# A four-layer residual kernel: the first pair's projections in 27 slots for 31, and two key batches asked for at other slots

## The chip, the cores and the metric

The kernel runs on one core of one Trainium2 chip. The metric is the device time of one execution in microseconds (us), and a lower time is better. All arithmetic is in 32-bit floats. The engines are called by short names: PE is TensorE, DVE is VectorE, ACT is ScalarE, POOL is GpSimd, and SP is SyncE, which here only issues transfers.

## What is computed

The input x has 64 batches of 32 rows of 512 columns (2048 rows in all). Four layers each add their result to x:

```python
x = x + _L0_cond_ref(x, itok_B_0_15, L0_cond_weights)       # mixes the 32 rows of a batch by one of 16 matrices
x = x + _L1_cond_ref(x, itok_B_6_15, base_weight, base_bias, lora_A_w, lora_B_w)   # linear, with a low-rank part
x = x + _L2_cond_ref(x, Wq, Wk, Wv, Wo, q_norm_w, k_norm_w, k_cache, v_cache, block_table, cache_seqlens)
x = x + _L3_cond_ref(x, L3_cond_weights, itok_B_0_15)       # mixes rows again
```

L2 is attention with a paged cache. Cut to what matters:

```python
q = rope(rmsnorm(x @ Wq.T))          # 32 heads of 128
k = rope(rmsnorm(x @ Wk.T)); v = x @ Wv.T      # 8 heads of 128
k_all = concat(k_cache[block_table], k)        # 512 cached keys (16 pages of 32) and 32 new ones
scores = q @ k_all.T / sqrt(128), cached keys from cache_seqlens on masked
out = softmax(scores) @ v_all, then @ Wo.T
```

Four query heads share one key head.

## The kernel before

The 2048 rows are 16 tiles of 128 rows (four batches each). The eight key heads are two groups of four. A step is one tile of one group, so there are 32 steps. A unit is one batch of a step, so there are 128 units, and each unit has four slots, one for each key head. A slot is the clock in which the program is written out: slot 0 is the first softmax slot, slot 511 the last, and slots -42 to -1 hold the first stage. Inside a slot a fixed order of parts is run (`slot`): "fetch" and "pool" first, then the scores of this slot's head, the products with values of the slot three before, the transposes of the probabilities of the slot two before, then "out", "pe", "take", "late", "power", up to three pieces of the norms (`norm_piece`), "turn", "dve", "keep", "act" and "store". A call is entered into the plan with `at(slot, part, function)`. Engines do not wait for slots: each runs its own queue in this order and waits only for what its instruction needs, so that the slot sets the order of the work and not its time.

The first stage (L0 and L1) runs tile by tile, two slots a tile: `home` is the tile's first slot. At `home` x is turned and mixed on PE (`turn_x`, L450, tile x1T_ps), at `home + 1` come the low-rank part (`ranks`, L465, h_ps) and three of five matmuls of L1 (`linear`, L481, l_ps), at `home + 2` the last two and the addition of the bias on DVE (`add`, L429), at `home + 3` the result is transposed (`turn_out`, L434, x2T_ps) and stored. For every second tile the sums of two tiles that the projections need (`sums`, L507 to L511, tiles x_12 and x_34) are made at `home + 4` on DVE and stored at `home + 5` (`store_sums`, L528, xS). The stores of the last three tiles go through POOL's queue, those before through SP's.

Projections take two tiles (a pair) at once, by a scheme of seven products for eight. For each pair there are three blocks: one for keys and values (KV), two for queries. A block has seven products of two matmuls each (`Block.project`, L664, 128x512, tile proj_ps, or a scores buffer s_ps for some of the first pair's), and a tuple of 14 slots says when each matmul is issued. There is one proj_ps buffer, so a product can start only when DVE (`add`, L676) or ACT (L684, the first product of a block) has taken the one before. Four results of a query block and two of the KV block go through a norm and a rotation: ACT squares them (L720), POOL takes a power (L725, L727), DVE does four pieces (`scale` L732, `straight` L739, `swapped` L751, `sum` L761), PE turns the heads (`turn`, L766, head_ps) and ACT keeps them (L778) as qT or kT_new. The value results are stored to memory (`store_values`, L706, vn) through SP's queue. `norm_piece` hands out the DVE pieces: at most two to a slot, three in every fourth, less what the takes and the block sums (`block_sum`, L628) have booked in `busy`.

For each unit SP asks for the 16 key pages (`Unit.__init__`, L796 to L804, kT, two buffers, 16 transfers of 64 KB), after having loaded the page numbers into registers. POOL makes the mask of the unit (`mask`, L819, tile pen) and gathers four tiles of values (L105, v_sb). The scores (L848, L851) go to the one s_ps buffer that the scores have; one instruction of DVE masks them and takes the maximum (L856), ACT does the exponential (L867) and a scaling (L873), PE transposes (L890, pT_ps), DVE copies (L892) and PE multiplies with the values (L900, o_ps).

The memory pools of the first stage are closed at slot -2 (`first.close()`), and the pools of the softmax (among them pen and v_sb) are opened in their place. The pool of the turned cache pages (`start_pool`) is closed a slot before the first keys are asked for, and the key buffers are opened there.

The variable `home` in the projections' loop is 32*(i-1) - 1 for pair i, so -33 for pair 0 and -1 for pair 1. The second part of the kernel, the product with Wo and L3, is not touched.

## Time and profile before

| | us |
|---|---|
| three timed runs | 2434.95, 2435.93, 2442.22 |
| median | 2435.93 |
| profiled execution, its own time | 2435.27 |
| its span, first to last instruction | 2433.5 |
| first matmul of PE starts | 10.00 |
| first scores (slot 0) start | 178.64 |
| scores of slot 4 and slot 8 start | 193.19 and 207.28 |

The page gives each engine's busy time and its share of the span, and cuts the span into 40 slices of 61 us, so the first stage fills slices 1 to 3. The waits list, for an engine, what it waited for with the total, the number of waits and the longest, in us. The timeline gives instructions in order of time: start, duration, engine, line, operation, what it writes and reads, and in brackets the idle time of the engine before it with what ended it. "SPq" rows are transfers being issued by SP: their duration is the issue's, not the transfer's. Two matmul instructions with one result show as x2; their ends are modelled, and the next one can start about 0.16 us before the end that the row shows. That drain counts as idle time when the next matmul has to wait.

### The profile page before, as it was taken

How to read it: one execution, taken by the hardware profiler on the slowest of the kernel's cores; microseconds unless marked ns; L12 is line 12 of the kernel's file. 1: busy time of each engine (PE TensorE's matmuls, PEld its weight loads, DVE VectorE, ACT ScalarE, POOL GpSimd, SP SyncE). 2: the span in 40 equal slices, each digit the busy share in tenths (PEclk: the TensorE clock that was granted, in tenths of full speed). 3: DMA queues.
4: the chain of work that ended last, by engine and by line, in shares of the span. 5: the costliest groups of instructions: out<-in, count | busy, mean ns of one | idle time of the engine just before them, and what ended most of it. 6: DMA issues, size and time to landing. Idle time of an engine off the chain costs nothing.

```text
span 2433.5 us, 47110 instructions
## 1 busy us (share of the span) xinstructions
PE 2398.2 (99%) x13792; PEld 1864.7 (77%) x13792; DVE 1651.9 (68%) x3555; ACT 1398.8 (57%) x4006; POOL 1230.5 (51%) x1269
## 2 busy tenths in 40 slices
PE   7999999999999999999999999999999999999999
PEld 4557777777777777777777777777777788888887
DVE  5557877777777777887777777777777856333222
ACT  2246767777777777777777777777676764000000
POOL 3336566655655666665656656666656663000000
PEclk9999999999999999999999999999999999999999
DMA  8766666676767677766666666566667874333221
GB/s 278 255 219 198 192 191 197 190 205 187 207 182 208 181 218 235 242 186 192 177 187 176 186 174 190 176 185 179 187 182 223 259 249 152 109 114 126 87 90 59
DMA packets 461055, 452.09 MB, mean 186 GB/s; under 512 B 67728, under 2 KB 383760, under 8 KB 457216
## 3 DMA queue, kind: packets, MB, share of 16 engines
q1 hardware_dynamic: 404960, 269.05, 36.7%
q0 software_dynamic: 55024, 179.25, 24.3%
q8 instruction: 111, 1.82, 0.3%
q14 instruction: 144, 1.18, 0.2%
q10 hardware_dynamic: 816, 0.79, 0.1%
HBM read 380.73 MB, written 76.55 MB: 188 GB/s over the span
## 4 chain that ended last, share of the span: by engine, by line
PE 93%; DMA 2%; ACT 1%; DVE 1%; issue 1%; SPq 1%; POOL 0%; ACTq 0%; DVEq 0%; POOLq 0%
PE proj_ps L664 23%; PE o_ps L900 18%; PE out_ps L1360 15%; PE s_ps L848 10%; PE pT_ps L890 9%; PE s_ps L851 9%; PE head_ps L766 3%; PE l_ps L481 3%; PE o_ps L913 1%; DMA o<-oT 1%; PE s_ps L883 1%; PE x1T_ps L450 1%; PE h_ps L465 1%; PE proj_ps L1174 1%; PE mix_ps L1378 1%
## 5 line engine op out<-in xcount | busy, mean ns | idle before, releaser
L105 POOL DMA_INDIRECT v_sb<-v,v_rows x512 | 544.4, 1063 | 357.1 <-PE o_ps L900 244.2
L900 PE MATMUL o_ps<-pT,v_sb 128*128 128x128 f32 x4096 | 623.8, 275 | 0.4 <-DMA v_sb<-v,v_rows 0.4
L900 PEld LDWEIGHTS o_ps<-pT,v_sb 128*128 128x128 f32 x4096 | 578.0, 191 | 27.4 <-DMA v_sb<-v,v_rows 0.6
L867 ACT ACTIVATE sm<-sm,top 128x544 f32<-128x544 f32 x512 | 380.9, 744 | 344.3 <-DVE top L856 341.5
L856 DVE CUSTOM_DVE_ANT_0 sm<-s_ps,pen 128x544 f32<-128x544 f32 x512 | 369.4, 722 | 111.5 <-PE s_ps L851 105.0
L873 ACT ACTIVATE sm<-sm,share 128x512 f32<-128x512 f32 x512 | 369.9, 722 | 100.2 <-DVE share L872 88.7
L892 DVE COPY pT<-pT_ps 128x512 f32<-128x512 f32 x512 | 353.3, 690 | 54.9 <-PE pT_ps L890 15.6
L848 PE MATMUL s_ps<-kT,qT 128*128 128x288 f32 x1024 | 334.5, 408 | 5.4 <-DMA kT<-kT 3.8
L890 PE MATMUL pT_ps<-ident,sm 128*128 128x128 f32 x2048 | 309.8, 274 | 4.6 <-ACT qT L778 3.1
L676 DVE TENSOR_TENSOR raw<-proj_ps,raw 128x512 f32<-128x512 f32 x332 | 224.4, 688 | 130.0 <-PE proj_ps L664 129.7
L851 PE MATMUL s_ps<-kT,qT 128*128 128x256 f32 x1024 | 304.7, 379 | 0.2 <-DMA kT<-kT 0.2
L848 PEld LDWEIGHTS s_ps<-kT,qT 128*128 128x128 f32 x1024 | 179.1, 190 | 152.7 <-issue 131.1
L819 POOL TENSOR_SCALAR pen<-key_f,seq_f 128x544 f32<-128x544 f32 x128 | 283.6, 2216 | 13.3 <-DMA kT<-kT 2.0
L890 PEld LDWEIGHTS pT_ps<-ident,sm 128*128 128x128 f32 x2048 | 238.7, 142 | 8.9 <-ACT qT L778 4.7
L720 ACT ACTIVATE sq<-raw 128x128 f32<-128x128 f32 x640 | 198.4, 310 | 74.9 <-DVE raw L676 59.8
L851 PEld LDWEIGHTS s_ps<-kT,qT 128*128 128x128 f32 x1024 | 194.5, 190 | 54.2 <-issue 0.6
L105 POOL DMA_INDIRECT mix_rows<-in_w,cond_rows x32 | 36.7, 1148 | 345.9 <-DVE mix_diag L170 299.8
L872 DVE RECIPROCAL share<-total 128x1 f32<-128x1 f32 x512 | 83.9, 164 | 181.1 <-ACT sm L867 167.0
L725 POOL TENSOR_SCALAR ss<-ss 128x4 f32<-128x4 f32 x160 | 39.4, 246 | 309.8 <-ACT sq L720 306.4
L1410 ACT COPY p<-out_ps 128x256 f32<-128x256 f32 x7 | 2.6, 372 | 333.1 <-PE out_ps L1360 333.1
L664 PE MATMUL proj_ps<-sum,x 128*128 128x512 f32 x380 | 188.0, 597 | 0.0
L727 POOL TENSOR_TENSOR rstd<-ss,minus_half 128x4 f32<-128x4 f32 x160 | 168.5, 1053 | 13.3
(175 smaller groups left out, 3570.7 us busy)
## 6 DMA issues: line engine op xcount, KB each, us to landing
kT<-kT SPq DMA_DIRECT2D x2048, 64.0 KB
o_in<-o SPq DMA_DIRECT2D x28, 1024.0 KB
o<-oT POOLq DMA_DIRECT2D x69, 256.0 KB, 3.0
o<-oT SPq DMA_DIRECT2D x58, 256.0 KB
v<-in_kv_cache SPq DMA_DIRECT2D x32, 256.0 KB
kT<-page_rows SPq DMA_DIRECT2D x32, 256.0 KB
vn<-raw SPq DMA_DIRECT2D x32, 256.0 KB
v_sb<-v,v_rows POOLq DMA_INDIRECT x512, 4.3
```

The source lines that it names most:

```text
L105: nc.gpsimd.indirect_dma_start(out=dst, out_offset=None, in_=table, in_offset=bass.IndirectOffsetOnAxis(ap=index, axis=0),)
L664: nc.tensor.matmul(self.ps, lhsT=self.pair.x[x][:, c if x == "b" else half.start + c, :], rhs=blocks(self.b)[w][:, c, :], start=(c == 0), ...
L819: nc.gpsimd.tensor_scalar(self.pen, key_f, seq_f[:, self.b : self.b + 1], BIG, ALU.is_ge, ALU.mult)
L848: nc.tensor.matmul(ps[:, first:HID], lhsT=q, rhs=self.kT[:, :n1, k, :], start=True, stop=True)
L851: nc.tensor.matmul(ps[:, HID : first + LA], lhsT=q, rhs=self.kT[:, n1:, k, :], start=True, stop=True)
L856: nc.vector.tensor_tensor_reduce(out=sm, in0=ps[:, first : first + LA], in1=self.pen, scale=1.0, scalar=3e38, op0=ALU.add, op1=ALU.min, ac ...
L867: nc.scalar.activation(sm, sm, AF.Exp, bias=top, scale=-1.0, accum_out=total)
L873: nc.scalar.activation(sm[:, :L], sm[:, :L], AF.Copy, scale=share)
L890: nc.tensor.transpose(ps[:, c, :], self.sm[k][:, c * P : (c + 1) * P], ident)
L892: nc.vector.tensor_copy(pT, ps)
L900: nc.tensor.matmul(o_of[self.s, k][:, self.j, :], lhsT=self.v[c][:, k * D : (k + 1) * D], rhs=self.pT[k][:, c, :], start=(self.j == 0 and ...
L1360: nc.tensor.matmul(ps[:, :HALF], lhsT=o[:, i, :], rhs=w[i // REP][:, i % REP, :], start=(i == 0), stop=(i == KG * REP - 1),)
```

## The change

The change does five things.

- The 14 matmuls of each block of pair 0 are laid into nine slots (`DENSE`) for ten, and the blocks begin 9 slots after each other, so that the first pair's projections take slots -33 to -7, where they took -33 to -3. One block sum is made at slot 14 of the pair for 17.
- The KV block of pair 1 begins two slots earlier, at slot -3, and still ends at slot 8.
- Up to slot -5, three norm pieces may run in a slot, where two or three could.
- The L1 of tiles 10 to 15 is one slot later, so the last tile's `home` is -8 for -9.
- The first unit's keys are asked for at slot -8 for -6, the second unit's at slot -1 for -3. The pool of the turned pages is closed two slots earlier with it.

```diff
         def norm_piece(slot):
-            if not pieces or pieces[0][0] > slot or busy.get(slot, 0) >= 2 + (slot % 4 == 1):
+            room_for = 3 if slot < -4 else 2 + (slot % 4 == 1)
+            if not pieces or pieces[0][0] > slot or busy.get(slot, 0) >= room_for:
                 return
...
+        DENSE = (0, 0, 1, 1, 2, 3, 4, 4, 5, 6, 7, 7, 8, 8)
...
                 (0, (10, 11, 12, 12, 13, 14, 15, 15, 16, 17, 18, 18, 19, 20)),
                 (1, (21, 21, 22, 23, 24, 24, 25, 26, 27, 27, 28, 29, 30, 30)),
             ):
+                if i == 0:
+                    slots = [(0, 9, 18)[(KV, 0, 1).index(b)] + w for w in DENSE]
+                elif i == 1 and b == KV:
+                    slots = (-2, -2, -1, -1, 0, 1, 2, 3, 4, 5, 7, 8, 9, 9)
                 slots = [home + w for w in slots]
...
-                    (17, 0, 4),
+                    (17 if i else 14, 0, 4),
...
-        ready = -6
+        ready = -8
         for t in range(NT):
-            home = -WINDOW - AHEAD - 6 + 2 * t
+            home = -WINDOW - AHEAD - 6 + 2 * t + (t > 9)
...
-            at(KG * (u - 1) if u > 1 else ready + 3 * u, "fetch", make, unit_of, u, Unit, u)
+            at(KG * (u - 1) if u > 1 else (ready, -1)[u], "fetch", make, unit_of, u, Unit, u)
```

## The prediction

> **What bounds the kernel now.** I read the page's first two parts, then TensorE's waits, then the timelines of all queues around the place that the change touches.

> ```profile
> PE 2398.2 (99%) x13792; PEld 1864.7 (77%) x13792; DVE 1651.9 (68%) x3555; ACT 1398.8 (57%) x4006; POOL 1230.5 (51%) x1269
> PE   7999999999999999999999999999999999999999
> PEclk9999999999999999999999999999999999999999
> ...
> PE x1T_ps L450 <- DVE mix_diag L421: 10.0, 1, 10.0
> PE s_ps L848 <- DMA kT<-kT: 3.8, 2, 2.2
> PE pT_ps L890 <- ACT qT L778: 3.1, 6, 1.6
> PE proj_ps L664 <- DVE raw L676: 1.6, 1, 1.6
> ```

> TensorE (PE) is busy for 99% of the span at full clock, and the change takes no matmul away. So it can only fill or open holes in PE's queue. In program order nothing differs behind about slot 10, some 40 us after the first scores (178.64 to 218.00). What counts is the idle time up to there: 10.0 us before the first matmul (untouched) and small holes, most of them near the first scores.

> ```profile
> 163.63 1.02 PE L481 MATMUL l_ps<-b_rows,hT 128*128 128x512 f32 x2
> 170.30 0.63 PE L766 MATMUL head_ps<-ident,rot_a 128*128 128x128 f32 x4 [0.48 <-DVE rot_a L761]
> 174.27 1.98 PE L664 MATMUL proj_ps<-wv,x_a 128*128 128x512 f32 x4 [1.62 <-DVE raw L676]
> 178.64 0.72 PE L848 MATMUL s_ps<-kT,qT 128*128 128x288 f32 x2 [1.66 <-DMA kT<-kT]
> 181.34 0.75 PE L848 MATMUL s_ps<-kT,qT 128*128 128x288 f32 x2 [0.68 <-DVE top L856]
> 186.79 0.63 PE L890 MATMUL pT_ps<-ident,sm 128*128 128x128 f32 x4 [1.37 <-issue]
> ...
> 173.07 1.08 POOL L528 DMA_DIRECT2D xS<-x  x2
> 178.39 2.12 POOL L819 TENSOR_SCALAR pen<-key_f,seq_f 128x544 f32<-128x544 f32 x1 [2.00 <-DMA kT<-kT]
> ...
> 166.85 10.16 SPq L804 DMA_DIRECT2D kT<-kT  x16
> 178.21 9.95 SPq L804 DMA_DIRECT2D kT<-kT  x16
> 193.14 9.79 SPq L804 DMA_DIRECT2D kT<-kT  x16
> ```

> Columns: start, duration, instruction, and in brackets the idle time before it with what ended it. E is the moment when PE is through with the last tile's L1: 163.63 plus two issues of 0.43, 164.49. Slot 4's scores start at 193.19, E+28.70. PE's work between, by start-to-start distances of the rows (projection matmul 0.86, four transposes 0.44, a score pair 0.92, a tile of o_ps or pT_ps 0.44): 14 projections 12.04, 5 head turns 2.20, x2T 0.44, four scores 3.68, pT and o 1.76; 20.12 in all. **The holes are 8.58 us.** That is what the change can win here. From E back to the first projection (37.41) they are 2.6 us, 1.39 at 41.40 and 0.70 at 78.00 the only large ones, and from 193.19 to slot 8 (207.28) some 0.3.

> The pen (the mask) matters beside the keys: it lies in memory that the first stage gives up, and in program order it waits for every transfer of that stage, the two xS stores of the last tile latest. Its 178.39 is 4.8 us after the second store's issue (173.61), and the first softmax (DVE, 180.55) starts as it ends.

> **The change part by part.** Projections: Pair 0's 42 matmuls, with their takes (DVE, ACT), squares, powers, turns and two vn stores, come up to four slots earlier and end at slot -7. Before E there are then 7 more matmuls (6.02) and 3 more heads (1.32): 7.3 us moved, not saved. Between E and slot 4 there remain 9 projections 7.74, 3 heads 1.32, x2T 0.44, scores 3.68, pT and o 1.76: 14.94. The hole at 78.00 goes, as the product behind the double take gets a slot's work between. Against it, twice a product follows the one before over x1T alone (0.89) where drain, take and two handovers need 0.16+0.04+0.69+0.05 = 0.94; I take 0.15 each. Dense stage: -0.4, with ends -0.7 and (five such holes of 0.7) +2.8. The earlier block sum (4 at 14 for 17) and the third piece a slot only reorder DVE, which is 50 to 60% busy there by the page's slices; cost nothing while that holds.

> L1 of tiles 10 to 15 a slot later: No projection now follows tile 15's last L1 matmul, so PE meets DVE's chain naked. Times from E, DVE steps by the rows 174.14 to 176.85 (straight 0.60, swapped 0.78, sum 0.61, scale 0.72; a rotation 2.71): the add runs 0.20 to 0.88, x2T starts at 0.93 (hole 0.94). The rest of one rotation (0.78, then 0.67) ends at 2.26: head at 2.31 (hole 0.94). A whole rotation more ends at 5.0: head at 5.05 (hole 2.30). Pair 1's first value product 5.49 to 7.21; ACT's copy (0.59) has to empty the one proj_ps buffer, so the second starts at 8.12 (hole 0.91); head to 10.28; the take ends at 10.73 and lets the next product start at 10.78 (hole 0.50). First scores at 11.64, next product done at 13.42. Before, block 1's last products filled this stretch.

> Pen: DVE starts tile 15's sums at 6.25, behind those rotations (1.46 in the row at 170.68). POOL issues xS at 7.15 and 7.85. Landing: at most 4.8 as now, at least 3.0 (a 256 KB store from POOL's queue by the page's part 6); I take 4.2, between, because the first key batch no longer shares the engines. Pen 12.0 to 14.1, first softmax at 14.2 (13.0 to 14.8). [...]

> First slots: Second scores come 0.79 after the softmax starts (180.55 to 181.34). In the new order ACT's table load (1.28 at 178.26) stands behind the wait for the first maximum, where it ran beside the pen before; so the first exp, DVE's reciprocal and the second softmax behind it come 1.25 late: third scores at 4.6 after the first softmax, fourth at 6.8. The four gathers of values (POOL, 1.3 apart behind the pen, landing 4.5 after issue as 186.99 to 191.57) end at 8.65, beside it. Slot 4 follows 9.9 after the first softmax: **E+24.1** (22.9 to 24.7).

> Keys: The first batch is asked for at slot -8, past x_12's load on SP; it waits only for the page store of slot -11 and xT of tile 12, so it lands many us early and the 1.66 at 178.64 goes. The second batch comes to stand behind x_34, x_b and, in the order, pair 1's vn store, which waits for the take of 10.73. Store 0.55 and register loads 0.7: first request at 12.0, last page 11.8 later (166.85 to 178.64): E+23.8, just under 24.1, no cost. Behind it on SP stand rot_k (1.22), a page load 0.40, v_new 0.66, register loads and gaps some 1.0: third batch requested at 25.5, landed at **E+37.3**. PE reaches slot 8 at 24.1 plus 11.65 of work (four slots of scores, pT and o at 2.24, three products, one turn 0.11) = 35.75. Hole 1.5, now the latest thing; before, the batch of 193.14 had 2.4 us to spare. The fourth batch has over 2 us again.

> **Sum.** Dense stage -0.4. Up to slot 4, 24.1-14.94 = 9.2 of holes for 8.58: +0.6. To slot 8, 1.5 for 0.3: +1.2. Together +1.4: the key hole goes, and rotation, pen and third batch take its place. The profiled execution took 2435.27 (span 2433.5 and 1.8 around it): 2436.7. It lies 0.7 under the median of the runs, so in their terms **2437.3, about 2437**.

> [...]

> **Rivals.** The holes go and nothing takes their place: For it: the four largest (1.66, 1.62, 1.37, 0.68) hang on keys and takes that come earlier. Without key, take and head holes the gain is 1.66+1.62+0.48+0.54 = 4.3: about 2432. For over 0.3% (7.3 us) nearly all 8.58 must go; the pen and the softmax chain, untouched, speak against it.

> The key chain starves PE: Second and third batch hang on one late take, with SP's 13.5 us a batch against 11.65 of PE work. A batch's issue varied from 9.50 to 10.77; two at the slow end make slot 8 E+38.6, +2.7 in all. It passes 7.3 us only if the vn take slips by some 6 us more, because from slot 8 on four slots take 15.1 (207.28 to 222.41) and SP catches up: 2444 and above.

> The dense stage stalls: If five products there meet their buffer full for 0.7 each, +2.8 for -0.4: 2440 to 2441. Against it: before, only two such holes in 31 slots.

> No effect: Holes change places one for one: 2436, within my range.

> **How the numbers follow.** A measurement of this kernel tells from no change about 0.3%, 7.3 us. Forecast, with no effect, 0.60; holes gone 0.18 (0.06 of it beyond 7.3); key chain 0.14 (0.08 beyond); dense stalls 0.08 (0.04 beyond). Faster 0.06, same 0.82, slower 0.12. Range: quicker handovers than I strung together, -4.3 with the runs' own spread, 2431; slow batches and dense stalls together, +2.7 and +3.2, 2443.

> **What would show it.** Right: no key wait at the first score; a head turn near E+5 waiting over 1.5 us for rot_a; pen 4 to 5 us after the xS issue and the first softmax at its end; a key wait at slot 8. Wrong: PE holes from E to slot 4 under 6 us, or over 12; a clock below 1.000; differences behind 220 us.

## The result, and the profile after

The changed kernel took 2441.32 us (median of 20 runs, 2439.11 to 2445.30), the kernel before 2435.81 (20 runs beside it, 2433.36 to 2442.22). The ratio is 1.0022, with a 95% interval of 1.0015 to 1.0029: 5.5 us slower, between 3.7 and 7.1. That is inside the range of 2431 to 2443 and within the 0.3% that I called no change, but 4.3 us over my number, and the sign is certain. The profiled execution took 2439.78 (span 2438.0).

First the waits of PE on the page's list (total, number, longest), for the kernel after:

```profile
PE pT_ps L890 <- ACT qT L778: 4.3, 4, 2.7
PE head_ps L766 <- DVE rot_a L761: 2.9, 2, 2.1
PE proj_ps L664 <- DVE raw L676: 2.2, 2, 1.8
PE proj_ps L664 <- ACT raw L684: 1.9, 2, 1.2
...
PE s_ps L851 <- DMA kT<-kT: 1.2, 1, 1.2
...
PE aT_ps L434 <- ACT x_b L497: 0.7, 1, 0.7
```

The 3.8 us that the scores waited for keys in the kernel before were two waits. One, 1.66 at the first scores, is gone; the other, 2.16 at 1993.29, is 1.15 at 1998.06 here and lies far behind the change. Waits for rotation, takes and copies stand in place of the first. PE's timeline shows where (a row of the dense stage, then from the last tile's L1 to slot 4 those with a wait and those that the text uses, and last the longest wait, which comes late):

```profile
111.18 0.66 PE L434 MATMUL aT_ps<-ident,a_rows 128*128 128x128 f32 x4 [0.72 <-ACT x_b L497]
...
171.61 1.02 PE L481 MATMUL l_ps<-b_rows,hT 128*128 128x512 f32 x2
173.51 0.63 PE L434 MATMUL x2T_ps<-ident,x_sb 128*128 128x128 f32 x4 [0.88 <-DVE x_sb L429]
174.90 0.63 PE L766 MATMUL head_ps<-ident,rot_a 128*128 128x128 f32 x4 [0.77 <-DVE rot_a L761]
177.63 0.63 PE L766 MATMUL head_ps<-ident,rot_a 128*128 128x128 f32 x4 [2.10 <-DVE rot_a L761]
178.09 3.35 PE L664 MATMUL proj_ps<-wv,x_a 128*128 128x512 f32 x4
182.12 1.99 PE L664 MATMUL proj_ps<-wv,x_a 128*128 128x512 f32 x4 [0.68 <-ACT raw L684]
...
184.96 1.13 PE L664 MATMUL proj_ps<-sum,x 128*128 128x512 f32 x2 [0.42 <-DVE raw L676]
...
190.94 1.12 PE L664 MATMUL proj_ps<-sum,x 128*128 128x512 f32 x2 [1.82 <-DVE raw L676]
...
197.22 0.65 PE L848 MATMUL s_ps<-kT,qT 128*128 128x288 f32 x2
...
1960.03 1.07 PE L890 MATMUL pT_ps<-ident,sm 128*128 128x128 f32 x4 [2.67 <-ACT qT L778]
```

E, the end of the last tile's L1, is 171.61 plus two issues of 0.43, 172.47, and was 164.49. The first three holes behind it stand where I strung them, at E+1.04, 2.43 and 5.16; the next two come some 1.6 later than I said, at E+9.65 and 12.49. Between them one row has no hole and is still too long: the product at 178.09 took 3.35 us where the next one took 1.99. The windows around it say why. Each row is a stretch of 3.41 us: its length, then busy time and number of instructions of PE, its weight loads, DVE, ACT and POOL, then the granted clock of PE, the share of the transfer engines, GB/s.

```profile
171.53:174.95 3.42, 1.78 (x8) 0.69 (x7) 2.25 (x5) 2.15 (x10) 1.59 (x3) 1.00 0.88 302
174.95:178.36 3.41, 1.31 (x9) 1.03 (x10) 3.24 (x7) 0.65 (x2) 1.67 (x3) 1.00 0.63 235
178.36:181.77 3.41, 3.08 (x4) 0.67 (x2) 3.31 (x8) 0.81 (x2) 1.08 (x2) 0.50 0.21 77
181.77:185.19 3.42, 2.65 (x9) 1.41 (x10) 0.69 (x1) 0.91 (x3) 1.49 (x1) 1.00 0.23 81
```

**Here PE ran one stretch of 3.41 us at half clock**, right behind a stretch in which it was busy for 1.31 of 3.41 us (0.38). The hole of 2.10 lies whole in that stretch; those of 0.88 and 0.77 lie in the one before it, in which PE was busy for 0.52. Up to slot 4 no hole was longer than 2.10.

This was not the only stretch at half clock in the execution. A second one, from 1960.11 to 1963.53, follows the hole of 2.67 at 1960.03, behind a stretch in which PE was busy for 0.22. In the kernel before the same wait, at 1955.87, took 1.56, and the clock stayed full.

Slot 4 starts at 197.22, E+24.75, and the softmax of slot 8 (DVE, L856) lags 3.13 us behind the kernel before. From there on program order is the same, and the lag stays between 2.1 and 3.6 up to 1830 us. It is still 3.06 at slot 484, grows to 5.83 at slot 485, behind the late hole of 2.67, and is 4.52 at the last softmax.

### The profile page after: what moved, and what is told of

Same layout as the page of the kernel before. It is cut to its first block, busy times and chain, and to the rows that moved or that the text cites. A ratio compares the mean times of both kernels' runs of the same rounds, so it can differ in the third digit from the quotient of the medians.

```text
span 2438.0 us, 47129 instructions
## 1 busy us (share of the span) xinstructions
PE 2401.6 (99%) x13792; PEld 1866.3 (77%) x13792; DVE 1652.5 (68%) x3555; ACT 1398.6 (57%) x4006; POOL 1228.9 (50%) x1269
## 2 busy tenths in 40 slices
PE   7999999999999999999999999999999999999999
## 3 DMA queue, kind: packets, MB, share of 16 engines
q8 instruction: 111, 1.82, 0.3%
## 4 chain that ended last, share of the span: by engine, by line
PE 93%; DMA 3%; ACT 2%; DVE 1%; issue 1%; SPq 0%; POOL 0%; ACTq 0%; DVEq 0%; POOLq 0%
PE proj_ps L664 23%; PE o_ps L900 17%; PE out_ps L1366 15%; PE s_ps L848 10%; PE pT_ps L890 9%; PE s_ps L851 8%; PE head_ps L766 3%; PE l_ps L481 3%; PE o_ps L913 1%; DMA kT<-kT 1%; DMA o<-oT 1%; PE s_ps L883 1%; PE x1T_ps L450 1%; PE h_ps L465 1%; PE mix_ps L1384 1%; ACT sm L867 1%
## 5 line engine op out<-in xcount | busy, mean ns | idle before, releaser
L856 DVE CUSTOM_DVE_ANT_0 sm<-s_ps,pen 128x544 f32<-128x544 f32 x512 | 369.3, 721 | 113.4 <-PE s_ps L851 107.5
L848 PE MATMUL s_ps<-kT,qT 128*128 128x288 f32 x1024 | 334.2, 408 | 1.6 <-ACT pT_new L885 1.6
L676 DVE TENSOR_TENSOR raw<-proj_ps,raw 128x512 f32<-128x512 f32 x333 | 225.0, 688 | 131.9 <-PE proj_ps L664 131.7
L890 PE MATMUL pT_ps<-ident,sm 128*128 128x128 f32 x2048 | 310.0, 274 | 4.5 <-ACT qT L778 4.3
L851 PE MATMUL s_ps<-kT,qT 128*128 128x256 f32 x1024 | 304.7, 379 | 1.2 <-DMA kT<-kT 1.2
L848 PEld LDWEIGHTS s_ps<-kT,qT 128*128 128x128 f32 x1024 | 179.5, 190 | 149.9 <-issue 127.4
L819 POOL TENSOR_SCALAR pen<-key_f,seq_f 128x544 f32<-128x544 f32 x128 | 282.9, 2210 | 13.8 <-DMA xS<-x 2.5
L890 PEld LDWEIGHTS pT_ps<-ident,sm 128*128 128x128 f32 x2048 | 239.2, 142 | 8.2 <-ACT qT L778 5.8
L851 PEld LDWEIGHTS s_ps<-kT,qT 128*128 128x128 f32 x1024 | 194.4, 190 | 55.4 <-ACT p_new L874 1.6
L664 PE MATMUL proj_ps<-sum,x 128*128 128x512 f32 x380 | 188.5, 597 | 2.2 <-DVE raw L676 2.2
```

The costliest lines, as they stand in the source:

```text
L664: nc.tensor.matmul(self.ps, lhsT=self.pair.x[x][:, c if x == "b" else half.start + c, :], rhs=blocks(self.b)[w][:, c, :], start=(c == 0), ...
L819: nc.gpsimd.tensor_scalar(self.pen, key_f, seq_f[:, self.b : self.b + 1], BIG, ALU.is_ge, ALU.mult)
L848: nc.tensor.matmul(ps[:, first:HID], lhsT=q, rhs=self.kT[:, :n1, k, :], start=True, stop=True)
L851: nc.tensor.matmul(ps[:, HID : first + LA], lhsT=q, rhs=self.kT[:, n1:, k, :], start=True, stop=True)
L856: nc.vector.tensor_tensor_reduce(out=sm, in0=ps[:, first : first + LA], in1=self.pen, scale=1.0, scalar=3e38, op0=ALU.add, op1=ALU.min, ac ...
L890: nc.tensor.transpose(ps[:, c, :], self.sm[k][:, c * P : (c + 1) * P], ident)
```

## The experiments

I held three explanations. The clock: the cluster of holes drops PE to half speed, some 1.5 us a stretch (3.35 us for a product that takes 1.88 at full clock) to 1.7 (half of 3.41, an estimate), in some runs more than once (the clock over the whole run is 0.9983 on average in the 20 runs of after and 0.9990 to 0.9991 in the runs of before listed below; 0.0008 of 2440 us is 2.0 us). The thin order: holes and late chains cost their own length, clock or not. The keys: SP's queue brings the second and third batch late. Twelve kernels ran in three groups of four; each group ran on one chip, beside the kernel before (28, 33 and 31 runs with medians 2437.08, 2434.72 and 2439.34), so ratios are to be compared across groups and times only within one. The changed kernel itself gave a ratio of 1.0022 at first and 1.0034 when it was repeated in the third group (e9); the first two groups hold no run of it. So a difference of some 0.001 between groups shows nothing by itself. In the table, the lag is that of slot 8's softmax in the profiled execution (208.69 in the kernel before).

| run | ratio to before (95%) | median | mean clock | lag at slot 8 |
|---|---|---|---|---|
| the change | 1.0022 (1.0015 to 1.0029) | 2441.32 | 0.9983 | 3.13 |
| e1, keys alone | 1.0004 (0.9995 to 1.0013) | 2438.51 | 0.9984 | 1.52 |
| e2, L1 later alone | 1.0019 (1.0010 to 1.0029) | 2441.12 | 0.9985 | 5.79 |
| e3, without L1 later | 1.0035 (1.0023 to 1.0048) | 2444.91 | 0.9975 | 11.36 |
| e4, old key slots | 1.0017 (1.0008 to 1.0026) | 2440.63 | 0.9977 | 7.31 |
| e5, unused products | 1.0025 (1.0016 to 1.0034) | 2441.36 | 0.9990 | 3.17 |
| e6, block moved back | 1.0007 (0.9998 to 1.0016) | 2437.52 | 0.9986 | 2.65 |
| e7, and sums, table | 1.0009 (1.0000 to 1.0018) | 2436.67 | 0.9985 | 1.86 |
| e8, table alone | 1.0030 (1.0019 to 1.0041) | 2441.42 | 0.9985 | 6.10 |
| e9, the change again | 1.0034 (1.0023 to 1.0045) | 2447.73 | 0.9976 | 6.26 |
| e10, before, keys, sums, table | 0.9999 (0.9990 to 1.0009) | 2437.77 | 0.9997 | -0.97 |
| e11, e7 and unused products | 1.0015 (1.0006 to 1.0024) | 2443.01 | 0.9990 | 1.78 |
| e12, e5 and e8 together | 1.0015 (1.0006 to 1.0025) | 2443.72 | 0.9992 | 2.95 |

### One part of the change alone, or one undone (e1 to e4)

e1 is the kernel before with `ready = -8` and the second batch at slot -1:

```diff
-        ready = -6
+        ready = -8
-            at(KG * (u - 1) if u > 1 else ready + 3 * u, "fetch", make, unit_of, u, Unit, u)
+            at(KG * (u - 1) if u > 1 else (ready, -1)[u], "fetch", make, unit_of, u, Unit, u)
```

> The kernel before with the two key requests alone moved (first batch at slot -8, second at -1). The key hole of 1.66 us at the first scores (178.64 in the profile before) should go. Theory that the keys were a bound of their own: the whole 1.66 comes back, 0.9993 of the time, about 2434. Theory that pen and first softmax gate the same slots (the pen of 178.39 waited for the last xS store as much as for keys): the scores come earlier, the first softmax at most 0.5 us, and the time stays within 0.5 us of the kernel before, 2435 to 2436. Theory that the second batch's place on the queue of SP starves PE: a key wait of 1 us or more at slot 4 or 8 and a time of 2437 or more.

The key hole went, and the scores of slot 1 waited 2.68 for the first softmax in its place, which the pen still holds back: one longer hole for two short ones. In the windows of e1 two stretches of half clock follow it (178.23 to 181.64 is the one with the hole):

```profile
178.23:181.64 3.41, 1.47 (x4) 0.30 (x2) 0.59 (x2) 1.76 (x2) 2.02 (x1) 1.00 0.40 101
181.64:185.05 3.41, 2.49 (x5) 1.85 (x6) 2.35 (x6) 1.77 (x4) 2.96 (x4) 0.50 0.59 154
185.05:188.47 3.42, 3.42 (x9) 2.09 (x8) 2.49 (x7) 2.24 (x5) 2.62 (x4) 0.50 0.68 187
```

The median is 1.4 us over before, with an interval that includes none. Asking for keys earlier gains nothing here, as the second theory said, but the clock does not stay up.

e2 is the kernel before with L1 of the last six tiles one slot later, e3 the changed kernel without it:

```diff
-            home = -WINDOW - AHEAD - 6 + 2 * t
+            home = -WINDOW - AHEAD - 6 + 2 * t + (t > 9)
```

> The kernel before with L1 of tiles 10 to 15 alone one slot later; the 31 slots of projections stay. PE's queue still holds block 1's last products beside tile 15's chain, so no cluster of holes there. Theory that the clock fell because PE had too little to do (1.13 of 4 us from 174 to 178 in the changed kernel): clock 1.000 here, the pen, and with it the first softmax, 1 to 2 us later, the time +1 to +2.5 against the kernel before, 2437 to 2438.5. Theory that the later L1 is by itself the whole loss: +4.5 to +5.5, about 2441, and a clock under 1.000. Theory that it is harmless: within 0.5 us of before.

e2 is 4.6 us slower (2.4 to 7.1) though it keeps 31 slots of projections. The pen starts at 184.17 for 178.39, and PE waits for the softmax behind it. In the timeline of e2:

```profile
184.17 2.12 POOL L819 TENSOR_SCALAR pen<-key_f,seq_f 128x544 f32<-128x544 f32 x1 [3.84 <-DMA kT<-kT]
...
187.11 1.07 PE L848 MATMUL s_ps<-kT,qT 128*128 128x288 f32 x2 [3.49 <-DVE top L856]
```

A stretch of half clock follows there too (from 187.41). Some 1.9 us of its lag is another matter: its first cache page came late (PE waited 2.23 at 19.20) and a stretch of half clock followed at once. The late L1 alone therefore costs nearly what the whole change costs.

> The changed kernel with L1 of tiles 10 to 15 at its old slots; the 27 slots and the key requests stay. If the late L1 made the loss: back to 2435 to 2436, the holes of 0.72 at 111.18 and 2.10 at 177.63 gone. If the 27 slots themselves thin PE's queue: holes of 1 us and more remain somewhere between slots -7 and -3, the clock can fall there too, and the time is 2438 to 2441. I expect some of both: 2437 to 2440, the dense stage shorter by 0.6 us or more than in the changed kernel.

I missed here: without the late L1 the 27 slots are no better than with it. The ratio is 0.0013 (3.2 us) over the first measurement of the change and level with its repeat. On e3's own chip e4, which has the late L1 but also other key slots, took 4.3 us less. DVE's timeline of e3 shows what is late there:

```profile
174.90 0.69 DVE L676 TENSOR_TENSOR raw<-proj_ps,raw 128x512 f32<-128x512 f32 x1 [3.93 <-PE proj_ps L664]
175.51 0.68 DVE L429 TENSOR_TENSOR x_sb<-l_ps,bias_sb 128x512 f32<-128x512 f32 x1
```

PE ends the last tile's L1 at 172.99 there, but the last products of pair 0 now follow it, and DVE takes them first in its queue. So the addition that everything hangs on starts at E+2.52, where it started at E+0.20 in the change. Holes of 1.03, 2.09 and 2.17 follow at 176.34, 179.06 and 181.85, then three stretches of half clock in a row from 181.00 and one from 198.06. (Some 2.1 us of e3's lag are a late first cache page, as in e2.) Without those 2.1 its lag at slot 8 is still some 9.2, where the two profiles of the change have 3.13 and 6.26. So with 27 slots the late L1 looks like the better of two bad places, but the medians do not prove it.

> The changed kernel with the key requests at their old slots (-6 and -3). Theory that the new place of the second and third batch costs time (the third term of my sum, +1.2): the time falls by 1 us or more, to 2440 or less, and slot 8's scores come earlier than E+37.9. Theory that holes and clock around slot -4 set the loss and the keys do not bind: the same as the changed kernel within 0.5 us (about 2441), clock under 1.000 in the same stretch, unless the first batch, asked for later, opens a key wait at the first scores, which then costs what it measures (at most 1.7).

In e4, the changed kernel with the key requests back at -6 and -3, the median is 0.0005 under the change in ratio, well inside both intervals. The profile has four stretches of half clock (three from 176.55, one from 193.62), three more than the change, which at up to 1.7 us each (the same estimate) can account for its larger lag (7.31 for 3.13), and no key wait up to slot 4. By the medians the keys' place alone does not decide.

### Filling the holes (e5, e8, e12)

e5 adds products that nobody reads, 4 in slot -5 and 10 in slot -4; e8 adds an exponential that nobody reads, which loads ACT's table early; e12 has both.

```diff
             run(i, "late")
+            if i in WARM:                                    # e5, e12: {-5: 4, -4: 10}
+                idle = ps_a.tile([P, P], F32, name="idle_ps", tag="tx")
+                for _ in range(WARM[i]):
+                    nc.tensor.matmul(idle, lhsT=ident, rhs=ident, start=True, stop=True)
...
             run(i, "act")
+            if i == -3:                                      # e8, e12
+                table_of = small.tile([P, 1], F32, name="top")
+                nc.scalar.activation(table_of, minus_half, AF.Exp)
```

> The changed kernel plus 14 products of the identity with itself on TensorE (0.22 us each, result unused) in slots -5 and -4, in front of the holes at x2T and the turn of slot -4; nothing else moves. The profiles so far show the clock fall in blocks of 3.41 us, each time after a block of 3.41 us with TensorE busy for less than some 0.46 (0.38 before the fall at 178.36 in the changed kernel). Theory of the clock: the blocks between 170 and 185 stay above 0.46, the clock stays 1.00 there, and the median falls by one block's loss and somewhat more, 1.7 to 2.5 us: 2438.5 to 2440, with fewer runs at clock .998 and below. Theory that the holes' own length is the whole loss: no change (2441), or +0.3 for dummies that overhang the holes.

> The changed kernel with one unused exponential on ACT in slot -3 and nothing else, so that the table load (1.28) stands ahead of the wait for the first maximum. My step said that its place behind the wait makes the first exponential 1.25 late, and with it slot 4. If that holds: the hole of 1.82 at 190.94 falls to 0.6, no second fall of the clock after it, slot 4 at E+23.5 in place of E+24.75, 1.0 to 1.8 us less: 2439.5 to 2440.5. The fall of the clock at 178 stays. If not: the same as the changed kernel.

By the ratio neither gained anything, and their profiles say why. In e5 the stretch behind 178 stays at full clock: the product that took 3.35 in the change takes 1.88, in the timeline of e5.

```profile
177.88 1.88 PE L664 MATMUL proj_ps<-wv,x_a 128*128 128x512 f32 x4
```

The first softmax comes 1.49 earlier than in the change. But the hole of 1.82 at the table load is still there, and now the clock falls behind that (and twice more late in the profile, from 1961.17 and from 1998.72). Windows of e5:

```profile
178.30:181.70 3.40, 2.72 (x7) 1.06 (x6) 3.16 (x8) 0.95 (x2) 1.08 (x2) 1.00 0.23 84
186.24:189.65 3.41, 1.39 (x5) 0.89 (x6) 1.18 (x5) 2.96 (x5) 2.67 (x3) 1.00 0.69 172
189.65:193.07 3.42, 3.42 (x7) 1.82 (x7) 0.54 (x3) 1.88 (x5) 3.05 (x2) 0.50 0.94 290
```

In e8 the hole at the table is 0.54 for 1.82, as my step said: from the first softmax to the fourth it takes 1.27 less than the change. But the clock fell at 178.65 for two stretches, and slot 4's scores waited 2.14 for a transfer. So I ran both together, and the changed kernel again beside it:

> The changed kernel itself once more, beside the next three runs. The profile taken first lags the kernel before by 3.1 us at the softmax of slot 8, of which some 1.65 is one block of half clock, and by 4.5 at the end, of which 1.4 comes in after 1900 us. If the parts in front of slot 8 are the change and the rest is chance: this profile lags by 1.5 plus 1.7 for each block of half clock at slot 8, and what comes later differs from the 1.4. Median 2440 to 2442.5.

> The changed kernel with the 14 unused products of slots -5 and -4 and the unused exponential of slot -3 together; in the run with the products alone the half clock moved to the block behind the hole of 1.82 at the first softmax, in the run with the exponential alone it stayed at 178. With both, no hole behind 20 us leaves a block under 0.46. If clock and table are the main loss: clock 1.000 in most runs, slot 8 within 1.0 of the kernel before, 2437.5 to 2439. If not: 2440 or more at clock 1.000, and the loss sits elsewhere.

On this chip the change takes 2447.73 and e12 2443.72: together the two edits bring 4.0 us of the 8.4 that the change costs there (the intervals of the two ratios just overlap). e12 has no stretch of half clock from 165 to 212, but it does not reach what I expected. Its timeline shows the next waits:

```profile
194.33 0.49 PE L900 MATMUL o_ps<-pT,v_sb 128*128 128x128 f32 x2 [0.71 <-DMA v_sb<-v,v_rows]
...
197.56 0.67 PE L851 MATMUL s_ps<-kT,qT 128*128 128x256 f32 x2 [1.39 <-DMA v_new<-vn]
```

The softmax of slot 3 lags 2.57 behind the kernel before (in the change 5.25), that of slot 4 already 3.96 (in the change 4.17). What PE gained it gives back to the gathered values and to a transfer on SP's queue. The same wait stands in e9; SP's queue and PE's timeline of e9:

```profile
185.44 0.32 SPq L706 DMA_DIRECT2D vn<-raw  x1
186.48 9.91 SPq L804 DMA_DIRECT2D kT<-kT  x16
...
198.50 0.65 SPq L826 DMA_DIRECT2D v_new<-vn  x1
```

```profile
197.72 0.65 PE L848 MATMUL s_ps<-kT,qT 128*128 128x288 f32 x2
199.67 0.67 PE L851 MATMUL s_ps<-kT,qT 128*128 128x256 f32 x2 [1.30 <-DMA v_new<-vn]
```

The bracket names v_new, but in the profile of the change the same L851 starts at 197.78, only 0.35 after v_new is asked for, so it cannot need it. L851 reads the second half of the second key batch, whose last request ended 3.28 before in e9 and 3.14 before in e12. That it is the keys is my inference. Of the five profiles with the second batch behind the vn store, the change has 0.07 of this wait, e5 none, e9 1.30, e12 1.39, e8 2.14 on L848.

### Putting work back into the stage (e6, e7, e11, e10)

e6 moves pair 1's first block back, e7 also puts tile 15's sums ahead of the rotations and loads the table early as e8 does (its exponential is not read), e11 adds 16 unused products in slot -3.

```diff
-                    slots = (-2, -2, -1, -1, 0, 1, 2, 3, 4, 5, 7, 8, 9, 9)
+                    slots = (-5, -5, -3, -3, 0, 1, 2, 3, 4, 5, 7, 8, 9, 9)     # e6, e7, e11
-                at(home + 4, "dve", call, *f, "sums")
+                at(home + 4, "dve" if t < NT - 1 else "power", call, *f, "sums")   # e7, e11, e10
```

> The changed kernel with pair 1's first block moved back into the holes: its products in slots -5 to 9 (-5, -5, -3, -3, 0, 1, ...) in place of -2, -2, -1, -1, 0, 1, .... The same work, in another order. Theory of the clock and of thin slots: the hole of 2.10 at 177.63 becomes 0.5 or less, the blocks stay above 0.46 up to the first softmax, and the wait moves to the first softmax, which the pen still gates: 1 to 2.5 us less than the changed kernel, 2439 to 2440.5. If the pen's chain takes all of it back as a wait of 3 us or more at the second scores (as in the run of the later L1 alone, 3.49), the clock falls there in its place and nothing is won: 2441 or more.

> As the run that moves pair 1's first block, and in addition tile 15's sums ahead of the rotations on DVE (so the xS stores and the pen come about 1.5 to 3 us sooner) and one unused exponential on ACT in slot -3, which loads the table (1.28) beside the pen. This takes out the two waits that follow the holes: the pen and the hole of 1.82 at 190.94. If these are the rest of the loss: 2436 to 2438, no more than 1 us over the kernel before or below it, clock .999 to 1.000. If the change's loss lies in the dense stage (+0.64) and elsewhere: 2439 and above.

e6 brings the ratio from 1.0022 to 1.0007 and e7 to 1.0009, the nearest to the kernel before of all versions of the change. On the same chip e5 and e8, which keep the change's order, took 3.8 to 4.8 us longer than e6 and e7. The hole did not vanish, it moved to the next turn (4.03 in e6, 4.16 in e7), and two stretches of half clock follow it in both. In return the take in front of the vn store comes earlier, SP asks for the second batch at 179.56 in e6 for 185.98, and no profile of this order shows a key wait at slot 4. e11 asks what the half clock costs by itself:

> The run that moves pair 1's first block, tile 15's sums and the table load, plus 16 products of the identity with itself on TensorE (result unused) in slot -3, where that run's profile has a hole of 4.16 us followed by two blocks of half clock (6.8 us). Nothing else differs, so this measures what the half clock costs by itself. Theory of the clock: no half clock between 180 and 190, two blocks or up to 3.4 us of loss gone less what the softmax chain gives back as waits: 1.5 to 3 us under that run, 2433.5 to 2435, clock .999 or better in most runs. If PE's slower clock there was hidden behind the pen: the clock rises and the time stays at 2436 to 2437.

The clock is 1.00 from 165 to 212 in e11. At the first softmax e11 is 1.42 ahead of e7, at slot 3 1.41, at slot 4 0.07: PE waits 1.08 for the gathered values, which come behind the pen, in both at about the same time (pen at 183.74 and 183.97). The timeline of e11:

```profile
183.74 2.12 POOL L819 TENSOR_SCALAR pen<-key_f,seq_f 128x544 f32<-128x544 f32 x1 [3.11 <-DMA kT<-kT]
...
194.84 0.49 PE L900 MATMUL o_ps<-pT,v_sb 128*128 128x128 f32 x2 [1.08 <-DMA v_sb<-v,v_rows]
```

By this profile the theory in which the half clock was hidden behind the pen holds for this order, and the ratio did not fall (1.0015 for 1.0009, intervals overlapping).

> The kernel before, not the changed one, with the key requests of the change, tile 15's sums ahead of the rotations on DVE, and one unused exponential in slot -3 for the table. With the keys alone moved the first scores came earlier and the second waited 2.68 for the softmax behind the pen; here the pen should come 1.5 us or more sooner too, so that wait falls to 1.5 or less and no block of half clock follows. If that holds: 1 to 3 us under the kernel before, ratio 0.9990 or so. If the pen is late for another reason, or the rotation that the sums now delay opens a hole of 1.5 at the head turns: the same as the kernel before, or up to 1 us over it.

e10 starts from the kernel before (its exponential is not read). Its profile is 0.97 ahead at slot 8 and 2.1 ahead at 1830 us, and its clock is the best of all, but the median does not differ from the kernel before within 0.1%. No version measured here beats it.

## Why the prediction was near, and which terms were wrong

The forecast was +1.4 us, and the measured difference is +5.5 (3.7 to 7.1): inside the range, and nearly four times the forecast. Two of my own signs of being wrong appeared, a clock below 1.000 and a difference behind 220 us (the lag that grows at 1960).

**The dense stage, -0.4: it was +0.64.** E moved by 7.98 us where 7.34 of work moved. The hole at 78.00 went, but I called the one-slot shift of L1 before E a mere reordering. In the new order the x2T of tile 9 stands right before the aT of tile 10 on PE (109.86 and 111.18), and aT waits for ACT's copy of x2T, 0.72 and the drain; e2, which has the late L1 alone, shows the same wait (0.67 at 112.16), e3 and the kernel before do not. Another wait of 0.29 came at 145.53. I had counted what the shift moves on DVE and not which two results share a buffer on PE.

**The holes from E to slot 4, 9.2: 9.81, but not the same ones.** Slot 4 came at E+24.75 for E+24.1. 1.47 of the 9.81 is the half clock (3.35 for the 1.88 that the same product takes in e5); the holes proper are 8.34, a little under the 8.58 of before: x2T 0.88 and drain for 0.94, the turn 2.10 and drain for 2.30, the second product 0.68 and drain for 0.91. The places and their causes are right, their sum is 0.9 smaller than the 9.2, and the clock puts 1.47 on top.

**The clock, priced at nothing: this is the term that I left out.** I counted every hole at its own length, the longest new one at 2.30, and gave the clock nothing in the sum; a clock below 1.000 stood only among the signs of being wrong. In the profiles the falls go with another quantity: the share of a 3.41 us stretch in which PE works. In the first profile the hole of 2.10 alone leaves 0.38 of its stretch, and the clock fell, with no idle time above 2.67 us anywhere behind the first matmul. In the repeat (e9) the stretches lie otherwise: the holes of 0.88 and 0.76 and the first 0.37 of the 2.10 fall into one, which leaves 0.41, and the clock fell there too. Windows of e9:

```profile
172.31:175.72 3.41, 1.41 (x9) 0.84 (x8) 3.15 (x6) 1.59 (x6) 2.53 (x4) 1.00 0.75 243
175.72:179.13 3.41, 1.68 (x5) 1.25 (x6) 3.24 (x8) 0.81 (x2) 0.72 (x2) 0.50 0.62 231
```

One stretch, not filled with work, cost PE 1.47 here, near the 1.7 that half of its 3.41 us gives as an estimate. What it costs at the end depends on what else is late: e5 and e11 ran that place at full clock and gained nothing in the median, and e12, with the table load out of the way too, was 4.0 us under the change.

**The table load behind the wait for the first maximum, 1.25: right.** ACT loads it at 187.94 for 1.28 us, and with it moved (e8) the hole falls from 1.82 to 0.54.

**Pen and first softmax, E+12.0 and E+14.2: E+11.2 and E+14.7.** The xS stores landed some 3.1 after the second issue (the pen starts at 183.70, the issues at 179.97 and 180.6), not 4.2. I had taken a middle between 3.0 and 4.8, and the lower end was the nearer one. The softmax did not profit: the scores, slowed by the clock, came last.

**The second key batch, "just under, no cost": a coin toss.** I put its landing 0.3 before slot 4. In the two profiles of the change it held once and failed once, by 1.30, if that wait is the keys' as I inferred. The mean of such a margin is not zero.

**The third batch, +1.2 at slot 8: the size is right by luck, the cause is not.** From slot 4 to slot 8 the change takes 13.19 us (197.22 to 210.41) for the 11.65 of work, 1.54 idle where I said 1.5. But the key wait that I named as a sign is not there: slot 4 came later, the batch landed in time, and 1.11 of the idle time is slot 6's wait at 204.10 for ACT's copy of pT_new.

The sum of +1.4 became +3.13 at slot 8 in the first profile: 0.64 dense, 1.47 clock, -0.24 the holes up to slot 4, 1.24 from there to slot 8, with 0.02 of rounding. The rival in which the key chain starves PE is partly true (slot 4 in the repeat, not slot 8); the rival in which the dense stage stalls is true in kind, with two new holes and not five; the rivals in which nothing takes the holes' place and in which nothing changes are refuted by the interval of the ratio.

What stays open: the median difference (5.5, and 8.4 in the repeat) is 2 us more than the lag at slot 8 in either profile. The repeat's lag of 6.26 has one stretch of half clock and one key wait more than the first. In the first profile 1.4 of it comes in at 1960: the hole of 2.67, where the kernel before has 1.56, and the second stretch at half clock add 2.77, and about half of that is won back by the end. PE waits there for ACT, and ACT for a store of o (1.95 for 0.85 before). This wait of PE varies from 1.26 (e2) to 3.40 (e11) over the 14 profiles. Half clock between 1950 and 2010 occurs in the change, e1, e2, e5 and e12, and neither in the kernel before nor in the repeat, so it is not shown to come from the change. Behind 1830 us, where all 14 profiled executions run the same instructions in the same order, the rest of the span took between 602.9 (e3) and 611.1 (e11), before 603.8, the change 605.2 and 606.2: this varies from one execution to the next by more than the effect, and single profiles can't settle the last 2 us. The version that would attack both chains at once, the second batch at slot -3 together with e12's two edits, was not run. Nor were the nine-slot blocks, the third norm piece and the earlier block sum run apart from each other.

## What to carry to other kernels

Judge PE's idle time by its busy share in short windows of the profile (here of 3.41 us) and not by the longest hole alone: in this kernel the clock fell behind one hole of 2.10 us that lay whole in a stretch, in the repeat behind a stretch with three holes of 0.76 to 2.10 or parts of them, in e1 behind one of 2.68 in the place of two shorter ones, and in e11 it did not fall behind one of 3.40. When two chains end within a microsecond of each other at the same slot, price the later of the two, with its spread, and expect an edit to one of them to bring nothing until the other is moved as well. When work is moved by a slot, read the new order on PE for neighbours that share a PSUM buffer (here x2T and aT, a wait of 0.72).

## What the runs showed of the hardware

In e3 half clock began at 20.57, 181.00 and 198.06; the distances are 47 and 5 times 3.413 us. In e2 it began at 20.15 and 187.41, 49 times 3.413 apart. The falls before 225 us lasted one to three such stretches (3.41 us in the change, 6.83 in e1, 10.24 in e3 from 181.00). Windows of e3, laid by its falls:

```profile
177.58:181.00 3.42, 0.63 (x4) 0.42 (x4) 3.26 (x7) 1.01 (x2) 2.52 (x4) 1.00 0.20 77
181.00:184.41 3.41, 2.56 (x6) 1.58 (x7) 3.25 (x7) 0.59 (x1) 1.08 (x2) 0.50 0.36 135
184.41:187.82 3.41, 2.73 (x4) 0.84 (x3) 1.53 (x4) 0.59 (x1) 1.29 (x1) 0.50 0.26 96
187.82:191.24 3.42, 3.42 (x7) 1.53 (x6) 0.33 (x1) 0.00 (x0) 2.83 (x3) 0.50 0.07 13
...
194.65:198.06 3.41, 1.59 (x5) 0.95 (x6) 1.25 (x3) 3.05 (x5) 2.84 (x3) 1.00 0.84 259
198.06:201.47 3.41, 3.41 (x9) 2.09 (x8) 0.62 (x4) 1.77 (x4) 0.49 (x1) 0.50 0.89 239
```
